# Storing the outputs of the last two quads plane by plane, from two DMA queues

## The chip, the cores and the metric

The kernel runs on one core of one Trainium2 chip. A core has five engines that run side by side, each with its own list of instructions in order: TensorE (PE in the profile, with PEld for its weight loads), VectorE (DVE), ScalarE (ACT), GpSimd (POOL) and SyncE (SP). Data goes between the chip's memory and the core through 16 DMA engines, which work off what SyncE's and ScalarE's queues hand them. The metric is the device time of one execution in microseconds, and lower is better.

## The reference

The input `x` is 128 samples of 64 channels by 1024 positions in float32; each sample has a style vector of 128. Four modulated convolutions of three taps are applied in turn (same length, upsampling by two with a blur, same length, blur and downsampling by two), and `x` is added to the result:

```python
def _layer(x, style, w, b, mw, mb, typ):
    s = style @ mw.T + mb
    weight = SCALE * w * s[:, None, :, None]
    demod = lax.rsqrt(jnp.sum(weight * weight, axis=(2, 3)) + EPS)
    weight = weight * demod[:, :, None, None]
    ...
out = x
for i, typ in enumerate(TYPES):        # same, upsample, same, downsample
    out = _layer(out, style, weights[i], biases[i], mod_w[i], mod_b[i], typ)
x = x + out
```

There is no nonlinearity between the layers, so away from the two ends of a sample all four are one convolution with its own weights for each sample.

## The kernel before

The kernel folds the four layers of a sample into one set of combined weights, built on TensorE from small products (`stage1`, `stage2`, `stage3`, lines 387 to 491), and then convolves each sample once. The three positions at either end of a sample are computed apart and leave by a store of their own (`Oe`, line 923).

Work is tiled by quads, four samples at a time, so there are 32 (`NQ`). Channels of two samples fill the 128 partitions, and two such pairs lie side by side. A sample's positions are split into three planes: plane `i` holds every third output, 340 of them. The convolution from three planes to three planes is done as five products instead of nine (`product`, line 579, and `conv0` to `conv4` that call it). They are accumulated in PSUM, in one pair of banks per quad (`psA`) and one that all quads share (`Y`), and VectorE puts them together (`sum1`, `sum2`, lines 627 to 641). Plane 1 is read from `y1w` in SBUF after `sum2`, plane 2 from `Y` after `conv4`, plane 0 from `psA` after `conv0`.

`output(q, i, s)` (line 651) scales plane `i` of pair `s`, adds the constant and writes it to the tile `o` of the quad in SBUF, on ScalarE (line 659) or VectorE (line 661). `store(q, s, planes, queue)` (line 663) is one DMA from `o` to the output, of as many planes as it is told; one plane of one pair is 170 KB, all three 510 KB. There are two `o` tiles, used in turn.

The order of work on each engine is the order in which the program is written: the schedule is a manual one, and the framework only adds the waits. The loop over quads begins at line 1101. An ordinary quad is convolved while the next quads' weights and inputs are prepared, and its two stores of 510 KB are issued by SyncE at the end of its turn (line 1224). The last two quads have branches of their own. Quad 30 is in the branch `n == NQ - 1` (line 1128): there planes 1, 2 and 0 of quad 30 are put out while `conv3`, `conv1` and `conv2` of quad 31 run in between. Quad 31 is in the branch `n == NQ` (line 1107), in which nothing is left to prepare; two of its outputs are given to VectorE to go beside ScalarE's.

Of the kernel before, what the change touches and what calls it, by code (L numbers as in the profile page):

```python
# [55 lines left out]
K = 3  # L56
# [7 lines left out]
def kernel(  # L64
# [9 lines left out]
    nc = tc.nc  # L74
# [8 lines left out]
    nc_v, nc_a, nc_g = nc.vector, nc.scalar, nc.gpsimd  # L83
# [344 lines left out]
    def stage2(q, pool=None, engs=(nc_a, nc_a), between=None):  # L428
        st = chain[q]
        ps = unit(pool or ps_w, f"psR{q}")  # L430
        for n, e in enumerate((-2, -1, 0, 1, 2, 3, 4, 5, 6)):
            if e % 2 == 0:
                a, lo, m = slice(1, 4), e // 2 + 1, 3
            else:
                a, lo, m = slice(4, 6), (e + 3) // 2, 2
            for r, rows in enumerate(HALF):
                for c, cols in enumerate(HALF):
                    src = st[c if r == 0 else 1 - c]
                    nc.tensor.matmul(  # L439
                        ps[r][cols, lo * C : (lo + m) * C],  # L440
                        E[rows, e + 2, :],
                        src[rows, a, :],
                        start=(n == 0),
                        stop=(n == 8),
                        skip_group_check=True,
                    )
        if between:
            between()
        rt = []
        for r in range(2):  # L450
            t = r_pool.tile([P, 7, C], F32, tag="R", name=f"R{q}_{r}")
            scaled_copy(
                engs[r], t.rearrange("c t o -> c (t o)"), ps[r][:, : 7 * C], tC[:, q, r : r + 1]
            )
            rt.append(t)
        chain[q] = rt
        return ps
# [79 lines left out]
    def t_tile(q, tag):  # L537
        if (q, tag) not in Ts:
            Ts[q, tag] = tpool.tile([P, 2, 1 + (tag != "T3"), PL], F32, tag=tag, name=f"{tag}_{q}")
        return Ts[q, tag]  # L540
# [31 lines left out]
    def in04(q, c):  # L572
        if q < NQ:
            t, g = t_tile(q, "T04"), Gs[q]
            a, b = g[:, c, :NJ], g[:, c, 2 * PL : 2 * PL + NJ]
            both = lambda v, step: bass.AP(v.tensor, v.offset, [list(v.ap[0]), [step, 2], [1, NJ]])
            nc_v.tensor_sub(t[:, c, :, :NJ], both(a, PL), both(b, 1))  # L577

    def product(q, m, ps, groups=range(K)):

        W, H_ = Wq[q]
        tag, i = SLOT[m]
        for g in groups:
            for s, rows in enumerate(HALF):
                for c, cols in enumerate(HALF):
                    if m in (0, 4):
                        w = W[rows, c, m // 2, g, :]
                    else:
                        w = H_[rows, m - 1, c, g, :]
                    nc.tensor.matmul(  # L590
                        ps[s][cols, :NB],
                        w,
                        Ts[q, tag][rows, c, i, g : g + NB],
                        start=(g == 0 and m == 3),
                        stop=(g == K - 1),
                        skip_group_check=True,
                    )
# [12 lines left out]
    def banks(q):  # L610
        return A[q] if isinstance(A[q], list) else [A[q][:, s] for s in range(2)]
# [31 lines left out]
    def conv4(q, *groups):  # L643
        product(q, 4, Y_banks, groups or range(K))

    def conv0(q, *groups):
        product(q, 0, banks(q), groups)
# [3 lines left out]
    def output(q, i, s, eng=nc_a):  # L651

        if q not in os:
            os[q] = opool.tile([P, 2, K, NB], F32, tag="o", name=f"o{q}")
        d3, add = td[:, q, s : s + 1], tb[:, q, s : s + 1]
        src = (banks(q)[s][:, :NB], y1w[q][:, s], Y[:, s, :NB])[i]
        dst = os[q][:, s, i]
        if eng is nc_a:
            nc_a.activation(dst, src, AF.Identity, bias=add, scale=d3)  # L659
        else:  # L660
            eng.tensor_scalar(dst, src, d3, add, op0=ALU.mult, op1=ALU.add)

    def store(q, s, planes=slice(0, K), queue=nc.sync):
        queue.dma_start(
            out[q, :, s, planes.start * NB : planes.stop * NB],
            os[q][:, s, planes].rearrange("c i j -> c (i j)"),
        )
# [108 lines left out]
    def zeros():  # L776
        for t in Ye:
            nc_g.memset(t[:, :, 0:1], 0.0)
            nc_g.memset(t[:, :, 7:8], 0.0)
        for t in Ue:  # L780
            nc_g.memset(t[:, :, 0:1], 0.0)
            nc_g.memset(t[:, :, 10:11], 0.0)
        for t in Ve:
            nc_g.memset(t[:, :, 0:2], 0.0)
            nc_g.memset(t[:, :, 10:12], 0.0)
        nc_g.memset(g1, 0.0)
# [314 lines left out]
    for q in range(NQ):  # L1101
        n, c, s = q + 1, q + 2, q + 3
        if q == 1:
            nc.sync.dma_start(Xe, x_ends)
        if q == 5:
            zeros()
        if n == NQ:
            conv4(q)
            for i in range(2):
                output(q, 2, i)  # L1110
            for i in range(2):
                output(q, 1, i, nc_v)
            for i in range(2):
                store(q, i, slice(1, 3))
            conv0(q, *range(K))
            for i, (eng, queue) in enumerate(zip(BOTH, (nc_a, nc.sync))):
                output(q, 0, i, eng)
                store(q, i, slice(0, 1), queue)
            break
        if c < NQ:  # L1120
            stage2(c)
        if n < NQ - 1:
            sum2(q)
        if n < NQ - 1:
            combine_a(n)
            combine_b(n)

        if n == NQ - 1:

            conv3(n, ps_w)  # L1130
            copy_m3(n)
            conv4(q, 0, 1)
            for i in range(2):
                output(q, 1, i)
            conv1(n)
            sum1(n)
            conv4(q, 2)
            for i in range(2):
                output(q, 2, i)
            in04(n, 0)  # L1140
            in04(n, 1)
            conv0(q, 0)
            conv2(n)
            conv0(q, 1, 2)
            sum2(n)
            for i in range(2):
                output(q, 0, i)
                store(q, i)
            continue

        conv4(q)
        if q == 0:
            var_matmul(PART[1], var_of(PART[1]), start=False)
            var_root(PART[1], var_of(PART[1]))
            var_inverse(PART[1])
            var_newton(PART[1])
            table_A(PART[1], dm[:, 2, PART[1]])
            for of in (table_C, vector_c0, table_3, vector_Da):
                of(PART[1])
        for i in range(2):  # L1160
            output(q, 2, i)
        if c < NQ:
            stage3(c, 0)
        conv3(n)
        copy_m3(n)
        in04(n, 0)
        in04(n, 1)
        if q:
            in3(c)
            in_g01(c, 0)  # L1170
            in_g01(c, 1)
        if c < NQ:
            stage3(c, 1)
        conv0(q, 0)
        conv1(n, 0)
        if q in SLOTS:
            slot(*SLOTS[q])
        elif s < NQ:
            stage1_a(s)
        conv1(n, 1, 2)  # L1180
        for i in range(2):
            output(q, 1, i)
        if q:
            in_g2(c)
            load(c + NX)
        if q and c < NQ - 1:
            in1(c, nc_g)
            in2(c, nc_g)
        if n == NQ - 2:
            combine_a(n + 1, lambda: sum1(n))  # L1190
            combine_b(n + 1)
        else:
            sum1(n)
        if q == 0:
            in_g01(c, 0)
            in_g01(c, 1)
        conv0(q, 1)
        if q in SLOTS:
            stage1_a(s)
        elif s < NQ:  # L1200
            stage1_b(s)
        conv0(q, 2)
        for i in range(2):
            output(q, 0, i)
        conv2(n, 0)
        if q in SLOTS:
            stage1_b(s, nc_v)
        extra(q, 0)
        extra(q, 1)
        if s + 1 < NQ:  # L1210
            scale3(s + 1)
        conv2(n, 1, 2)
        if n == NQ - 2:
            sum2(n)
            in1(n + 1, nc_v)
            in2(n + 1, nc_v)
        if q == 0:
            in_g2(c)
            in3(c)
            load(c + NX)  # L1220
            in1(c, nc_g)
            in2(c, nc_g)
        for i in range(2):
            store(q, i)
# [74 lines left out]
```

## Time and profile before

| | us |
|---|---|
| runs: median of 3 (lowest, highest) | 495.83 (495.58, 497.23) |
| the profiled execution | 496.51 |
| its span, first to last instruction | 494.7 |
| TensorE matmul busy | 481.8 |
| VectorE busy | 398.7 |
| ScalarE busy | 290.5 |
| GpSimd busy | 137.0 |

The profile is of one execution. Times inside it are microseconds from the start of its span; the execution's own time is 1.8 us longer than the span. Groups of instructions are named by the line of the kernel, the engine, the operation and what it writes and reads (`out<-o` is a store from the tile `o`). `SPq` and `ACTq` are the queues of SyncE and ScalarE: a DMA's row gives the time that its issue took there, and apart from it the time from issue to landing, when the last of the 16 DMA engines has reported its part. The DMA share is the mean busy share of the 16 engines. q1 carries what SyncE issues and q10 what ScalarE issues; the queues marked "instruction" carry program code to the engines.

### The profile page before, as it was taken

Reading aid. Unit: us, or ns where it says so; the run is one execution under the profiler, and the core shown is the slowest. Engines: PE = TensorE matmul, PEld = TensorE weight load, DVE = VectorE, ACT = ScalarE, POOL = GpSimd, SP = SyncE. Lnnn points to the kernel's source line nnn. Section 1 sums busy time; section 2 is a strip of 40 time slices with the busy share of each in tenths; the row PEclk is TensorE's granted clock in tenths of the full one; section 3 lists DMA queues with packets and bytes.
Section 4 is the critical chain, followed back from the end, with each engine's and each line's share of the span. In section 5 each row is a group of like instructions: output and inputs, shape, how many; then the busy total and the mean of one; then the engine's idle time right before and its main releaser. Section 6 shows DMA issues by size and latency. Waiting matters only on the chain.

```text
span 494.7 us, 22227 instructions
## 1 busy us (share of the span) xinstructions
PE 481.8 (97%) x10056; PEld 355.1 (72%) x10056; DVE 398.7 (81%) x704; ACT 290.5 (59%) x579; POOL 137.0 (28%) x164
## 2 busy tenths in 40 slices
PE   8999999999999999999999999999999999999994
PEld 6877687767777766767777777766766777777752
DVE  4986888798898869997768897759998768878783
ACT  5456646556565656556566556656555657566552
POOL 3544412344213223121223112223123323211200
PEclk9999999999999999999999999999999999999998
DMA  7220744443334442344443334442344442434224
GB/s 248 94 90 4 237 155 168 173 167 113 109 133 173 174 171 93 102 158 170 173 154 108 114 145 173 174 164 75 115 166 173 173 173 89 160 128 161 89 86 170
DMA packets 19727, 70.42 MB, mean 142 GB/s; under 512 B 2224, under 2 KB 2992, under 8 KB 19632
## 3 DMA queue, kind: packets, MB, share of 16 engines
q1 hardware_dynamic: 19408, 68.70, 39.0%
q8 instruction: 79, 1.29, 1.0%
q10 hardware_dynamic: 224, 0.29, 0.2%
q14 instruction: 16, 0.13, 0.1%
HBM read 35.36 MB, written 33.62 MB: 139 GB/s over the span
## 4 chain that ended last, share of the span: by engine, by line
PE 82%; DVE 11%; POOL 4%; issue 2%; ACT 1%; POOLq 0%; DVEq 0%
PE psA L590 37%; PE psR L439 14%; PE psW L480 13%; PE Y L590 9%; PE psS L369 5%; DVE G L501 3%; PE psE L820 2%; DVE H L501 2%; POOL T L565 1%; DVE T L577 1%; POOL T L570 1%; PE Y L169 1%; DVE Y L501 1%; DVE y L641 1%; DVE Wf L498 1%
## 5 line engine op out<-in xcount | busy, mean ns | idle before, releaser
L590 PE MATMUL psA<-T,H 64*64 64x340 f32 x2304 | 192.2, 446 | 0.7 <-DVE y L501 0.7
L565 POOL TENSOR_TENSOR T<-G 128x684 f32<-128x684 f32 x30 | 50.1, 1669 | 306.7 <-DVE G L501 266.6
L590 PEld LDWEIGHTS psA<-T,H 64*64 64x64 f32 x2304 | 92.8, 133 | 53.0 <-issue 6.7
L439 PE MATMUL psR<-S,E 64*64 64x192 f32 (+1 forms) x2304 | 88.0, 301 | 3.6 <-POOL S L425 2.3
L439 PEld LDWEIGHTS psR<-S,E 64*64 64x64 f32 x2304 | 77.3, 133 | 18.0 <-POOL S L425 7.6
L340 ACT ACTIVATE R<-psR,tC 128x448 f32<-128x448 f32 x63 | 36.6, 631 | 75.7 <-PE psR L439 73.9
L501 DVE SCALAR_TENSOR_TENSOR G<-X 128x688 f32<-128x688 f32 (+1 forms) x96 | 78.1, 866 | 0.0
L590 PE MATMUL psA<-T,Wf 64*64 64x340 f32 x768 | 74.0, 447 | 0.0
L501 DVE SCALAR_TENSOR_TENSOR y<-psA,m 128x680 f32<-128x680 f32 (+1 forms) x33 | 27.8, 845 | 46.8 <-PE psA L590 46.6
L340 ACT ACTIVATE Wf<-psW,t 128x384 f32<-128x384 f32 (+1 forms) x126 | 56.4, 498 | 11.5 <-PE psW L480 11.5
L480 PE MATMUL psW<-R,w0s 64*64 64x128 f32 (+1 forms) x1536 | 62.1, 287 | 0.4 <-ACT Wf L340 0.3
L590 PE MATMUL Y<-T,Wf 64*64 64x340 f32 x768 | 61.6, 446 | 0.4 <-DVE Y L501 0.3
L480 PEld LDWEIGHTS psW<-R,w0s 64*64 64x64 f32 x1536 | 51.1, 133 | 8.2 <-ACT Wf L340 1.2
L577 DVE TENSOR_TENSOR T<-G 128x684 f32<-128x684 f32 x64 | 52.7, 865 | 0.0
L659 ACT ACTIVATE o<-Y,tb,td 128x340 f32<-128x340 f32 x64 | 37.2, 631 | 23.4 <-ACT R L340 16.8
L570 POOL TENSOR_TENSOR T<-G 128x684 f32<-128x684 f32 x30 | 50.0, 1666 | 0.0
L369 PEld LDWEIGHTS psS<-wd,w2n 64*64 64x64 f32 x1160 | 38.5, 133 | 11.1
L659 ACT ACTIVATE o<-psA,tb,td 128x340 f32<-128x340 f32 x63 | 36.7, 634 | 14.9 <-PE psA L590 14.9
L590 PEld LDWEIGHTS Y<-T,Wf 64*64 64x64 f32 x768 | 31.8, 133 | 17.0 <-DVE Y L501 1.0
L340 ACT ACTIVATE S<-psS,tBn 128x256 f32<-128x256 f32 x58 | 24.4, 471 | 25.4 <-PE psS L369 25.3
L622 ACT COPY m<-psA 128x680 f32<-128x680 f32 (+1 forms) x33 | 23.3, 710 | 25.4 <-PE psA L590 25.4
L659 ACT ACTIVATE o<-y,tb,td 128x340 f32<-128x340 f32 x62 | 38.1, 668 | 0.0
(148 smaller groups left out, 529.2 us busy)
## 6 DMA issues: line engine op xcount, KB each, us to landing
X<-in_x SPq DMA_DIRECT2D x64, 516.0 KB, 4.5
out<-o SPq DMA_DIRECT2D x62, 510.0 KB, 4.4
out<-o SPq DMA_DIRECT2D x2, 340.0 KB, 4.4
Xe<-in_x_ends SPq DMA_DIRECT2D x1, 512.0 KB, 7.4
par<-in_params SPq DMA_DIRECT2D x2, 192.0 KB, 3.5
par_s<-in_params_s SPq DMA_DIRECT2D x1, 196.0 KB, 2.8
par<-in_params SPq DMA_DIRECT2D x2, 96.0 KB, 2.9
out<-Oe SPq DMA_DIRECT2D x1, 192.0 KB, 1.9
```

The source lines that it names most:

```text
L340: nc_a.activation(dst, src, AF.Copy, scale=f)
L369: nc.tensor.matmul(ps[r][cols, at * C : (at + n) * C], weight[rows], wd[c if r == 0 else 1 - c][rows, taps], start=first, stop=last, skip_ ...
L439: nc.tensor.matmul(ps[r][cols, lo * C : (lo + m) * C], E[rows, e + 2, :], src[rows, a, :], start=(n == 0), stop=(n == 8), skip_group_check ...
L480: nc.tensor.matmul(ps[r][cols, at : at + m * C], w0s[kind][rows, k, :], rt[c][rows, first : first + K * (m - 1) + 1 : K, :], start=(n == 1 ...
L501: nc_v.scalar_tensor_tensor(out, x, f, y, op0=ALU.mult, op1=op)
L565: eng.tensor_add(t[:, :, 0, :NJ], plane(g, 2), plane(g, 1))
L570: eng.tensor_sub(t[:, :, 1, :NJ], plane(g, 2), plane(g, 1))
L577: nc_v.tensor_sub(t[:, c, :, :NJ], both(a, PL), both(b, 1))
L590: nc.tensor.matmul(ps[s][cols, :NB], w, Ts[q, tag][rows, c, i, g : g + NB], start=(g == 0 and m == 3), stop=(g == K - 1), skip_group_check ...
L622: nc_a.copy(m3c[q][:, s], a)
L659: nc_a.activation(dst, src, AF.Identity, bias=add, scale=d3)
L820: nc.tensor.matmul(ps[r][cols, : HB * n].rearrange("c (b j) -> c b j", j=n), weight(i, r, c)[rows], moving(i, r, c)[rows], start=(i == 0), ...
```

## The change

In the branch of quad 30, planes 1 and 2 are stored as soon as both are written, and plane 0 alone at the end. In the branch of quad 31, plane 1 is put out and stored first in the program's order, one pair from SyncE's queue and one from ScalarE's; plane 2 is stored alone when it is written. Plane 0 of quad 31 goes as before. Before, quad 30 left in two stores of three planes, and quad 31 in two stores of two planes and two of one; now there are two stores of two planes and eight of one. No arithmetic is added or removed. TensorE, VectorE, GpSimd and ScalarE keep their instructions in the same order, except for one DMA issue that ScalarE gains ahead of its plane-2 outputs of quad 31.

```diff
         if n == NQ:
+            for i, queue in enumerate((nc.sync, nc_a)):
+                output(q, 1, i, nc_v)
+                store(q, i, slice(1, 2), queue)
             conv4(q)
             for i in range(2):
                 output(q, 2, i)
-            for i in range(2):
-                output(q, 1, i, nc_v)
-            for i in range(2):
-                store(q, i, slice(1, 3))
+                store(q, i, slice(2, K))
             conv0(q, *range(K))
             for i, (eng, queue) in enumerate(zip(BOTH, (nc_a, nc.sync))):
                 output(q, 0, i, eng)
@@
             conv4(q, 2)
             for i in range(2):
                 output(q, 2, i)
+                store(q, i, slice(1, K))
             in04(n, 0)
             in04(n, 1)
             conv0(q, 0)
@@
             sum2(n)
             for i in range(2):
                 output(q, 0, i)
-                store(q, i)
+                store(q, i, slice(0, 1))
             continue
```

## The prediction

> **What bounds the kernel now.** I read the page's head and its chain first, to see which engine carries the span. The last line is from the chain of waits in order of time, over the last 30 us.
>
> ```profile
> span 494.7 us, 22227 instructions
> PE 481.8 (97%) x10056; PEld 355.1 (72%) x10056; DVE 398.7 (81%) x704; ACT 290.5 (59%) x579; POOL 137.0 (28%) x164
> PE 82%; DVE 11%; POOL 4%; issue 2%; ACT 1%; POOLq 0%; DVEq 0%
> ...
> 488.30 0.63 DVE o L661
> ```
>
> TensorE is the bound for all but the end. The chain's last piece of arithmetic ends at 488.30 + 0.63 = 488.93, while the span is 494.7: 5.8 us pass in which nothing is computed. The edit touches nothing before 481 us, so this tail is the stage to price. Next I read the end of the waits of SyncE's queue, then the instructions of the kernel's closing line.
>
> ```profile
> SPq L1290 <- DMA out<-o: 4.3, 1, 4.3
> ...
> L1290 SPq EVENT_SEMAPHORE  x7: 17/28/4322, 489.3 to 494.7; - x7
> ```
>
> SyncE waits 4.32 us, from 489.34 to about 493.65, for the last store to land; the remaining 494.7 - 493.65 = 1.05 us is the closing handshake, which the edit leaves alone. So the span moves one for one with that landing. The stores' own rows (windows on the last two stores, on the two before them, on the pair of quad 30, and the lone side store) say why it takes so long:
>
> ```profile
> L664 ACTq DMA_DIRECT2D out<-o x1: 378/378/378, 488.9 to 488.9; - x1
> L664 SPq DMA_DIRECT2D out<-o x1: 332/332/332, 489.0 to 489.0; - x1
> DMA to landing us min/median/max: 4.5/4.6/4.7
> ...
> L664 SPq DMA_DIRECT2D out<-o x2: 401/588/776, 487.3 to 488.1; - x2
> ...
> L664 SPq DMA_DIRECT2D out<-o x2: 332/332/332, 485.2 to 485.7; - x2
> ...
> out<-Oe SPq DMA_DIRECT2D x1, 192.0 KB, 1.9
> ```
>
> A last store of 170 KB takes 4.5 to 4.7 us, though the side results' store of 192 KB, alone on the DMA engines, landed after 1.9. The difference is a queue: six stores (2 x 510, 2 x 340, 2 x 170 = 2040 KB of 1024 bytes) are issued within 3.8 us. The table of stretches shows the DMA engines (columns: stretch, length, busy time of PE, PEld, DVE, ACT, POOL, clock, DMA share, GB/s):
>
> ```profile
> 480.00:485.20 5.20, 5.13 (x75) 3.42 (x70) 4.31 (x9) 1.82 (x4) 0.00 (x0) 1.00 0.00 0
> 485.20:485.75 0.55, 0.55 (x13) 0.34 (x9) 0.55 (x3) 0.50 (x1) 0.00 (x0) 1.00 0.00 0
> ...
> 486.00:491.00 5.00, 2.22 (x32) 1.09 (x24) 0.63 (x1) 1.80 (x3) 0.00 (x0) 1.00 0.99 381
> 490.50:491.50 1.00, 0.00 (x0) 0.00 (x0) 0.00 (x0) 0.00 (x0) 0.00 (x0) 0.96 0.95 343
> 491.89:492.87 0.98, 0.00 (x0) 0.00 (x0) 0.00 (x0) 0.00 (x0) 0.00 (x0) 0.50 0.07 22
> 492.90:493.60 0.70, 0.00 (x0) 0.00 (x0) 0.00 (x0) 0.00 (x0) 0.00 (x0) 0.50 0.00 0
> ```
>
> From 480.0 to 485.75 they move next to nothing; from 486.0 to 491.0 they are full at 381 GB/s. Then from 491.89 to 492.87 their share is 0.07, about one engine of sixteen, carrying 22 GB/s x 0.98 us = 21.6 kB, a sixteenth of the last two stores: one engine runs over a microsecond behind the others. What made it late stands in the rows of the DMA queues, over 485.70 to 485.80 and over the span:
>
> ```profile
> q8 instruction: 1, 0.02, 90.9%
> ...
> q8 instruction: 79, 1.29, 1.0%
> q14 instruction: 16, 0.13, 0.1%
> ```
>
> One packet of program code starts in that 0.1 us; 90.9% of 16 engines x 0.1 us is 1.45 us on one engine. Its start is in the 23rd of 40 slices, 485.76, so this engine is free at 487.21 and has its share, 2040 KB/16 = 130.6 kB, done at 492.87: 5.66 us, 23 GB/s. The landing follows 0.78 us behind its last packet. That is the whole tail: a backlog, worked off last by the engine that fetched code.
>
> **The change, part by part.** The rows of ScalarE and VectorE that make the planes ready, in order of time:
>
> ```profile
> 480.97 1.16 ACT L659 ACTIVATE o<-Y,tb,td 128x340 f32<-128x340 f32 x2 [1.51 <-PE Y L590]
> 484.54 1.16 ACT L659 ACTIVATE o<-psA,tb,td 128x340 f32<-128x340 f32 x2 [2.41 <-PE psA L590]
> 485.16 0.82 DVE L661 TENSOR_SCALAR o<-y,td,tb 128x340 f32<-128x340 f32 x2
> 486.61 1.16 ACT L659 ACTIVATE o<-Y,tb,td 128x340 f32<-128x340 f32 x2 [0.91 <-ACT o L659]
> 488.24 0.63 ACT L659 ACTIVATE o<-psA,tb,td 128x340 f32<-128x340 f32 x1 [0.47 <-PE psA L590]
> ```
>
> 1. Quad 30, planes 1 and 2 (2 x 340 KB): plane 2 is ready at 480.97 + 1.16 = 482.13, and plane 1 was before it. The stores now issue at about 481.6 and 482.2 instead of with plane 0 at 485.20 and 485.73. The 0.8 us from issue to first packet is the time from 485.20 to 486.0; 696 kB at 381 GB/s take 1.83, so they run from 482.4 to 484.3 in the stretch that showed no traffic. SyncE was waiting there anyway. Matmuls, weight loads and outputs go on as before; their cover is that the matmuls already ran beside full DMA engines from 486.0 on.
>
> 2. Quad 30, plane 0 (2 x 170 KB): the issues stay at 485.20 and 485.73, with a third of the bytes.
>
> 3. Quad 31, plane 1 (2 x 170 KB): ready at 485.16 + 0.82 = 485.98, instead of waiting for plane 2 at 487.2 and 487.8. SyncE issues one behind its two others, 0.53 after 485.73, at 486.26; ScalarE issues the other at 486.0. Its issue is the one instruction added to a compute engine. Priced by the issues that ScalarE and SyncE show, it takes 0.38; the longest of all output issues took 1.08 (row below). Behind it stand ScalarE's plane-2 outputs, which began at 486.61, and then the last one, at 488.24 after 0.47 of idle time. An issue of 0.38 ends at 486.38 and costs nothing; one of 1.08 ends at 487.06, puts the outputs 0.45 back and eats the 0.47 to the last hundredths. I take zero, bound 0.05. Without that cover all of it would be on the end.
>
> ```profile
> L664 SPq DMA_DIRECT2D out<-o x65: 332/344/1080, 50.1 to 489.0; - x65
> ```
>
> 4. Quad 31, plane 2 (2 x 170 KB): issued at 487.27 and about 487.8 as it is ready. Plane 0: ScalarE at 488.91, SyncE at 488.96, as now. SyncE's two extra waits in front of it end at 488.2 at the latest.
>
> The bytes left behind the code packet are then 8 x 170 KB = 1360 KB, on the late engine 87.0 kB. Rows of one plane go slower than whole ones: 343 GB/s at share 0.95 is 22.6 GB/s for each engine, so 3.85 us, and from 487.21 the last packet ends at 491.06. Nothing holds it up on the way: the last stores' packets are there from 488.96 + 0.8 = 489.8, when this engine still has two stores' worth before it. Landing 0.78 later: 491.84, against 493.65. **The sum is -1.8 us.**
>
> Bounds. If that engine is not late at all, the last pair itself sets the end: the lone side store took 1.9 us, of which 196.6 kB / 385 GB/s = 0.5 were transfer, so 1.35 are fixed; 488.96 + 1.35 + 348 kB / 361 GB/s (0.96) = 491.3, a gain of 2.4. The mean code packet of that queue is 1.0% x 16 x 494.7 / 79 = 1.0 us, shorter than 1.45, so the gain is pulled towards this end rather than away. The other way: a second code packet (the smaller kind, 0.1% x 16 x 494.7 / 16 = 0.5 us) on the same engine leaves 1.3. I take 1.8, from the engine as it stood here. A fixed cost per store would come on top; the six stores here already fit their bytes (23 GB/s on the late engine, 22.6 with one-plane rows alone), so I take none.
>
> The profiled execution took 496.51 us, 1.8 around its span, so it would take 494.7. It stands 0.7 above the median of the runs, 495.83; the same sum on the median gives **494.0 us** (-0.36%).
>
> On this cost the Trainium skill speaks against the change. "DMA: Bandwidth & Descriptors", section "Bandwidth", says to batch transfers to a megabyte or more, and measures 0.95 us for 64 KB and 6.15 for 1 MB (loads issued from GpSimd); between them that is an estimated 0.6 us per transfer beside its bytes. The sum by it would be two more stores behind the code packet, 1.2 us, and a gain of 0.6. The trace here does not agree: with 0.6 each, the last two one-plane stores would have held the late engine for 1.2 us beside their bytes, and it took 0.98 with them. It is the third rival's rule, in a milder form.
>
> **The rivals.**
>
> *A part of the gain is lost, or it drowns.* An engine is late again at another moment, by 0.3 us or more beyond the 1.45, and 0.3 to 1.8 of the gain is gone: 494.3 to 495.8, by its middle 495.2. For it: code packets fall where they fall, and runs of one kernel already lie 495.58 to 497.23 apart, as wide as the gain. Against it: TensorE's code is untouched, and with it the place of this packet.
>
> *The change does not do what it says.* A store lands about 4.5 us after its issue whatever is queued; the last issues stay, and so does the time: 495.8. For it: the median of all the output stores is 4.4. Against it: those travel in pairs of 510 KB, mostly beside loads, and the lone store landed in 1.9.
>
> *A fixed cost per store: slower.* Place: the late engine's queue, between 487.21 and the end. Each of the eight stores costs c more than its bytes at the rates above, so the end moves by 8c against a gain of 1.8; at c = 0.23 the gain is gone, above it the kernel is slower, at 0.41 by 0.3%. The upper price is the 1.35 us of the lone store, if it could not overlap with the next one: 8 x 1.35 - 1.8 = 9 us, 504.8. Against it: the last two one-plane stores, one from each queue, passed the late engine in 0.98 us together, all included, and 0.96 is what I give a pair. At the smallest price that counts, c = 0.41, it would be 497.3.
>
> **How the numbers follow.** About 0.3% (1.5 us) is what a measurement here can tell from no change. The forecast (gain 1.5 to 2.4): 0.66; part of the gain lost: 0.24; no effect: 0.06; fixed cost: 0.04. The forecast's own range is 493.4 to 494.4. For 8 in 10 I go from 493.0 (gain 2.4 and 0.4 for the spread of runs) to 495.5, which takes in most of the lost gain. Faster by over 0.3%: 0.66; within: 0.30; slower: 0.04.
>
> **What would show it.** Right: traffic between 482.4 and 484.3; ScalarE's added issue done before 486.6 and its last output at 488.24 as before; issues of the last two stores at 488.9; from issue to landing 2.9 instead of 4.7; SyncE's last wait 2.5 instead of 4.32. Wrong: a later last output (the added issue held ScalarE), a landing still 4 us after issue with the queue empty (it was no backlog), or a new stretch with one busy engine long after the others (code fetched later).

## The result: faster by a fifth of a percent, half of what was forecast

| | before | after |
|---|---|---|
| median of 22 runs (lowest, highest), us | 496.40 (495.18, 497.79) | 495.17 (494.53, 496.47) |
| ratio after to before, 95% interval | | 0.9981 (0.9974 to 0.9989) |
| profiled execution, us | 496.51 | 494.94 |
| its span, us | 494.7 | 493.1 |

The ratio on record is a gain of 0.94 us on 496.4 (0.55 to 1.29); the two medians lie 1.23 apart, a quotient of 0.9975. The forecast was 1.8, with 1.5 to 2.4 as its own range. The gain is clear of zero, but it lies under the forecast's range and under the 0.3% that the prediction took as the least that can be told from no change. That 495.17 lies inside the wide range of absolute times, 493.0 to 495.5, says little.

The head of the profile after shows that nothing but the end has moved: all five engines do the same work, within 0.7 us. The arithmetic ends at the same moment too, by the last line of its chain of waits, in the second fence: 488.28 + 0.63 = 488.91, before 488.93.

```profile
span 493.1 us, 22234 instructions
PE 481.8 (98%) x10056; PEld 354.4 (72%) x10056; DVE 398.4 (81%) x704; ACT 290.6 (59%) x579; POOL 136.6 (28%) x164
```

```profile
488.28 0.63 DVE o L661
```

The rows of the last two stores of the profile after, and those of the other late stores between 485.1 and 488.5:

```profile
L664 ACTq DMA_DIRECT2D out<-o x1: 360/360/360, 488.9 to 488.9; - x1
L664 SPq DMA_DIRECT2D out<-o x1: 332/332/332, 488.9 to 488.9; - x1
DMA to landing us min/median/max: 3.0/3.1/3.2
...
L664 SPq DMA_DIRECT2D out<-o x5: 332/406/1152, 485.2 to 487.9; - x5
L664 ACTq DMA_DIRECT2D out<-o x1: 354/354/354, 486.0 to 486.0; - x1
```

The last store lands 3.2 us after its issue instead of 4.7. One number stands out: an issue on SyncE that took 1.152 us, against 0.33 for most (the longest of the late ones before took 0.776). It is the plane-1 store that stands right behind ScalarE's added one. The stretches of the profile after (columns as in the prediction):

```profile
482.40:484.30 1.90, 1.90 (x30) 1.30 (x22) 1.44 (x4) 0.00 (x0) 0.00 (x0) 1.00 0.95 367
486.00:487.00 1.00, 1.00 (x20) 0.69 (x16) 0.00 (x0) 0.41 (x1) 0.00 (x0) 1.00 0.88 310
487.00:487.50 0.50, 0.50 (x16) 0.29 (x11) 0.00 (x0) 0.50 (x2) 0.00 (x0) 1.00 1.02 348
487.50:488.00 0.50, 0.50 (x12) 0.10 (x4) 0.00 (x0) 0.25 (x1) 0.00 (x0) 1.00 0.51 174
488.00:489.00 1.00, 0.19 (x4) 0.00 (x0) 0.63 (x1) 0.63 (x1) 0.00 (x0) 1.00 0.98 343
489.00:490.00 1.00, 0.00 (x0) 0.00 (x0) 0.00 (x0) 0.00 (x0) 0.00 (x0) 1.00 0.59 203
490.00:491.00 1.00, 0.00 (x0) 0.00 (x0) 0.00 (x0) 0.00 (x0) 0.00 (x0) 0.76 0.75 263
491.00:491.65 0.65, 0.00 (x0) 0.00 (x0) 0.00 (x0) 0.00 (x0) 0.00 (x0) 0.50 0.06 21
```

Quad 30's early planes do travel from 482.4 to 484.3. But from 486 on the DMA engines are no longer full: 0.51 for half a microsecond at 487.5 and 0.59 in all of 489 to 490, where before the share was 0.99 throughout. The second gap is only a wait for the last pair: its issues are at 488.9, and first packets come 0.8 us behind an issue. And one engine is still last: from 491.0 to 491.65 the share is 0.06, about one engine of sixteen.

### The profile page after: what moved, and what is told of

Same layout as the page of the kernel before. It is cut to its first block, busy times and chain, and to the rows that moved or that the text cites. A ratio compares the mean times of both kernels' runs of the same rounds, so it can differ in the third digit from the quotient of the medians.

```text
span 493.1 us, 22234 instructions
## 1 busy us (share of the span) xinstructions
PE 481.8 (98%) x10056; PEld 354.4 (72%) x10056; DVE 398.4 (81%) x704; ACT 290.6 (59%) x579; POOL 136.6 (28%) x164
## 3 DMA queue, kind: packets, MB, share of 16 engines
q8 instruction: 79, 1.29, 1.1%
## 4 chain that ended last, share of the span: by engine, by line
PE 82%; DVE 11%; POOL 4%; issue 2%; ACT 1%; POOLq 0%; DVEq 0%
PE psA L590 37%; PE psR L439 14%; PE psW L480 13%; PE Y L590 9%; PE psS L369 5%; DVE G L501 3%; PE psE L820 2%; DVE H L501 2%; POOL T L565 1%; DVE T L577 1%; POOL T L570 1%; PE Y L169 1%; DVE Y L501 1%; DVE y L641 1%; DVE Wf L498 1%
```

## The experiments

Two theories stood against each other. *Backlog*, the prediction's: the end moves with the bytes that are queued behind the code packet. *Feeding*: many small stores reach the DMA engines more slowly than their bytes, because issues are held or two queues disturb each other.

The arithmetic itself ends anywhere from 488.3 to 490.6 us in the profiles of these kernels, though none of the edits but the last product's order and the start's warm-up touches it. That scatter is as large as the effect, so beside the timed ratio I read each trace's *tail*: from the end of the last output to the last landing. It is the end of the last output in the chain of waits, the issue right behind it, and the "DMA to landing" of that issue. Each ratio compares runs on one chip; the tails are single profiles, and the three groups of experiments below ran on three chips.

### Each half alone, one queue, and the change again

The half in quad 30 alone is the change with quad 31's branch left as it was:

```diff
         if n == NQ:
-            for i, queue in enumerate((nc.sync, nc_a)):
-                output(q, 1, i, nc_v)
-                store(q, i, slice(1, 2), queue)
             conv4(q)
             for i in range(2):
                 output(q, 2, i)
-                store(q, i, slice(2, K))
+            for i in range(2):
+                output(q, 1, i, nc_v)
+            for i in range(2):
+                store(q, i, slice(1, 3))
```

> Only the half of the change in quad 30: planes 1 and 2 leave early, plane 0 at the end; quad 31 is stored as before the change (two stores of two planes, two of one, six in all behind 485 us instead of eight). Backlog theory (the end moves with the bytes queued behind the code packet, 1360 KB as in the full change): the same time as the full change, the last landing near 491.8 to 492.2, about 1.5 us less than before in the profile. Feeding theory (eight small stores reach the DMA engines more slowly than their bytes, and two issuing queues get in each other's way): faster than the full change by 0.3 us or more, and the DMA share stays at 0.95 or above between 487 and 490.

The half in quad 31 alone is the kernel before with the opposite edit:

```diff
         if n == NQ:
+            for i, queue in enumerate((nc.sync, nc_a)):
+                output(q, 1, i, nc_v)
+                store(q, i, slice(1, 2), queue)
             conv4(q)
             for i in range(2):
                 output(q, 2, i)
-            for i in range(2):
-                output(q, 1, i, nc_v)
-            for i in range(2):
-                store(q, i, slice(1, 3))
+                store(q, i, slice(2, K))
```

> Only the half of the change in quad 31: plane 1 early, one pair from SyncE and one from ScalarE, plane 2 alone; quad 30 leaves whole at the end as before. Backlog theory: 2040 KB behind the code packet as before, so no difference from before (within 0.3 us). Feeding theory: the small stores cost time and buy nothing, 0.3 to 0.8 us slower than before.

One queue for both plane-1 stores:

```diff
-            for i, queue in enumerate((nc.sync, nc_a)):
+            for i, queue in enumerate((nc.sync, nc.sync)):
```

> The full change with both plane-1 stores of quad 31 issued by SyncE; ScalarE issues only its last store. Backlog theory: the same as the full change within 0.2 us. Feeding theory with the two queues in each other's way: the long issue on SyncE (1.15 us in the full change) is gone, issues follow at 0.53 us, and the end comes 0.3 to 0.6 us earlier than in the full change. If the small rows alone are the limit, the same as the full change.

> The full change once more, on the chip of the three halves: 0.9 to 1.3 us less than before. In its trace the theory of backlog expects the same places of the waits as in the first profile; if the long SyncE issue beside ScalarE's and the gaps of the DMA share at 487.5 and 489.5 are chance, they are gone or elsewhere.

| | ratio to before (95%) | tail, us |
|---|---|---|
| half in quad 30 | 0.9964 (0.9951 to 0.9977) | 3.22 |
| half in quad 31 | 1.0003 (0.9991 to 1.0016) | 4.97 |
| full change, one queue | 0.9984 (0.9971 to 0.9997) | 3.52 |
| full change again | 0.9980 (0.9969 to 0.9992) | 3.70 |

The half in quad 31 wins nothing, as the backlog theory expected (2040 KB stay behind the code packet); the 0.3 to 0.8 us of loss that the feeding theory expected is neither shown nor excluded by its time, whose interval goes up to 0.8, and its tail is 0.27 longer than the longest of before. The half in quad 30 carries the gain. Its 1.8 us are more than the full change's 0.94, as the feeding theory expected, but see its repetition below. No issue is held in it (0.33 us each). The theory's other sign, a DMA share of 0.95 or more between 487 and 490, did not come: it was 0.31 from 487 to 488, where the half's stores of two planes had only just been issued. The second queue is not what disturbs: with SyncE alone the time is the same, and a long issue is there too (1.13 us, on the fourth store in a row).

In the repetition of the full change the held issue is longer. Its rows of the late stores, and its stretches around the hold:

```profile
L664 SPq DMA_DIRECT2D out<-o x5: 332/384/1516, 485.5 to 488.6; - x5
L664 ACTq DMA_DIRECT2D out<-o x1: 354/354/354, 486.3 to 486.3; - x1
```

```profile
487.00:488.00 1.00, 1.00 (x20) 0.65 (x16) 0.00 (x0) 1.00 (x2) 0.00 (x0) 1.00 0.89 310
488.00:488.50 0.50, 0.50 (x8) 0.00 (x0) 0.00 (x0) 0.11 (x1) 0.00 (x0) 1.00 0.07 19
488.50:489.00 0.50, 0.06 (x4) 0.00 (x0) 0.35 (x1) 0.41 (x1) 0.00 (x0) 1.00 0.94 318
```

From 488.0 to 488.5 the share is 0.07, one engine of sixteen: fifteen have run dry and one works. So the gap behind a held issue is no chance. What was still open was whether the number of small stores holds the issue, or the one late engine.

### The floor, the number of stores, and the order of the last product

```diff
         if n == NQ:
-            for i, queue in enumerate((nc.sync, nc_a)):
+            for i in range(2):
                 output(q, 1, i, nc_v)
-                store(q, i, slice(1, 2), queue)
...
                 output(q, 2, i)
-                store(q, i, slice(2, K))
...
             for i in range(2):
                 output(q, 0, i)
-                store(q, i, slice(0, 1))
             continue
```

> Leaves work out: plane 0 of quad 30 and planes 1 and 2 of quad 31 are computed but never stored, so only the last pair of stores stands behind 485 us. It measures the end without any backlog. By the bounds of the prediction the last landing comes 2.3 us after SyncE's last issue and the time is 2.4 us under before. If the two last stores are worked off one behind the other, as the half in quad 30 showed (landings 0.55 us apart, the second 3.19 after its issue), 2.8 to 3.2 after the issue and 1.6 to 2.0 under before, the same as that half.

Split, from the half in quad 30:

```diff
             for i in range(2):
-                store(q, i, slice(1, 3))
+                store(q, i, slice(1, 2))
+                store(q, i, slice(2, 3))
```

> The half in quad 30 alone, but each of quad 31's two stores of two planes is split into two stores of one plane, issued one behind the other at the place of the whole one: same bytes, eight stores behind 485 us instead of six, rows of 1360 bytes instead of 2720, and nothing leaves earlier. Backlog theory: as the half in quad 30 alone (about 1.8 us under before). Feeding theory: issues held for 0.4 us or more, gaps in the DMA share, and 0.4 to 0.9 us slower than that half, about where the full change is.

By side, from the half in quad 30; `product` gets an argument that sorts its order of groups and pairs by pair:

```diff
-            conv0(q, *range(K))
-            for i, (eng, queue) in enumerate(zip(BOTH, (nc_a, nc.sync))):
+            product(q, 0, banks(q), range(K), True)
+            for i, (eng, queue) in enumerate(((nc_v, nc.sync), (nc_a, nc_a))):
```

> The half in quad 30 alone, with the last product of quad 31 ordered pair by pair instead of group by group: the first pair's plane 0 is finished about 0.9 us earlier, put out on VectorE and stored by SyncE, so that the last store goes alone, from ScalarE. If the last two stores being worked off one behind the other sets the end, 0.5 to 0.9 us faster than the half in quad 30 alone. If the landing behind the last issue is what it is whatever goes before, no difference.

> The half in quad 30 alone once more, beside the three above: 1.3 to 2.2 us under before. Where its code packet comes late or long in the trace, the backlog theory expects one engine behind the others at the end again; the feeding theory expects no held issue of SyncE in either case.

| | ratio to before (95%) | tail, us |
|---|---|---|
| floor: last pair alone | 0.9974 (0.9960 to 0.9987) | 3.09 |
| quad 30's half, quad 31 split | 0.9985 (0.9970 to 0.9999) | 3.64 |
| quad 30's half, last product by side | 0.9976 (0.9963 to 0.9989) | 2.89 |
| quad 30's half again | 0.9982 (0.9967 to 0.9997) | 3.19 |

The floor kernel leaves out the other six late stores. It is the surprise. The end of its chain, and then the rows of its last pair:

```profile
488.48 0.63 DVE o L661
```

```profile
L664 ACTq DMA_DIRECT2D out<-o x1: 379/379/379, 489.1 to 489.1; - x1
L664 SPq DMA_DIRECT2D out<-o x1: 332/332/332, 489.1 to 489.1; - x1
DMA to landing us min/median/max: 3.0/3.0/3.1
```

With nothing at all in front of them the last two stores still need 3.0 and 3.1 us to land. The prediction had 2.3 for this; of the two outcomes expected before this run, the second came. So no store moved out of the way can win more than about 4.7 - 3.1 = 1.6 us here, and quad 30's half, with tails of 3.22 and 3.19, is already there. The Trainium skill, "DMA: Bandwidth & Descriptors", section "Anatomy of one DMA", gives 2.0 us plus the bytes at 436 GB/s (measured on another issuing path); for the pair's 348 kB, taken as one transfer, that is an estimated 2.8, nearer to the 3.1 measured here than the prediction's bound.

The split was meant to have the same bytes at the same times as quad 30's half, but it has not. Plane 1 is written before plane 2, so the first of the split stores no longer waits for plane 2. SyncE issues it at 487.7, half a microsecond before ScalarE begins plane 2, where the half's store of two planes comes 1.5 us behind the store before it. That issue is held for 1.34 us:

```profile
L664 SPq DMA_DIRECT2D out<-o x2: 332/837/1342, 487.3 to 487.7; - x2
488.16 1.16 ACT L659 ACTIVATE o<-Y,tb,td 128x340 f32<-128x340 f32 x2 [0.91 <-ACT o L659]
```

So the tail, 0.42 to 0.45 longer than the half's, is no price for the number of stores alone. By side, the last store goes alone, and the tail is 0.30 shorter than quad 30's half, less than the 0.5 expected.

The timed ratios do not resolve all this. Quad 30's half came out at 0.9964 and then at 0.9982, in intervals that overlap, so that it is faster than the full change is not shown by its times; its tails (3.22 and 3.19 against 3.25 and 3.70) only suggest it. By side and quad 30's half both beat the kernel before; neither is told from the full change by its time.

### The kernel before again, and the code packet moved away

> The kernel before once more, for a second sample of its end: from the end of the last output to the last landing 4.70 us in its first profile. Backlog theory with the code packet: 4.4 to 4.9 again, one engine last by about 1.1 us at the landing, since the packet's place in TensorE's code does not change. If the first profile was an unlucky one, 3.7 to 4.2, which would by itself explain most of what the timed gain lacks.

> The kernel before a third time, for the spread of its tail: 4.4 to 4.9 by the backlog theory with the code packet; anywhere from 3.6 to 4.9 if the packet's length (0.9 to 1.9 us in the profiles so far) sets it, in step with that length.

For the two kernels with a shifted start, one edit in the warm-up at the start, made in the kernel before and in the full change:

```diff
-    zeros_to_y(2, 256)
-    zeros_to_y(2, 384)
+    zeros_to_y(20, 32)
```

> The kernel before, with the warm-up products at the start cut into more and narrower ones (20 sets of 32 columns instead of 4 of 256 and 384): 128 more instructions in TensorE's code, so its code packets fall about 4.5 us earlier against the work, and none falls between 485 and the end. Backlog theory with the code packet: the 15 punctual engines set the end, tail from the last output to the landing 3.6 us instead of 4.7. If the packet has nothing to do with the late engine, 4.7 again.

> The full change with the same narrower warm-up products. Without a late engine SyncE's issues should not be held (0.33 to 0.45 us instead of 1.15 and 1.52), and the tail should be at its floor, 3.0 to 3.2 us. Against the kernel before with the same start that is only 0.4 to 0.6 us, so most of what the change wins would be the late engine's backlog. If held issues come from the number of small stores and not from the late engine, they are held here too, and the tail stays 3.3 to 3.7.

The second profile of the kernel before: the end of its chain, SyncE's last store with the landings of the last pair, and the code packet, in the rows of the DMA queues over the 0.1 us from 487.05:

```profile
489.86 0.63 DVE o L661
```

```profile
L664 SPq DMA_DIRECT2D out<-o x1: 335/335/335, 490.5 to 490.5; - x1
DMA to landing us min/median/max: 3.8/4.0/4.2
```

```profile
q8 instruction: 1, 0.02, 73.6%
```

And the same of its third profile (the packet over the 0.1 us from 487.80):

```profile
489.99 0.63 DVE o L661
```

```profile
L664 SPq DMA_DIRECT2D out<-o x1: 332/332/332, 490.6 to 490.6; - x1
DMA to landing us min/median/max: 4.3/4.4/4.5
```

```profile
q8 instruction: 1, 0.02, 54.8%
```

Tails of 4.24 and 4.49: the 4.70 of the first profile is the longest of three, and their mean is 4.48. The 4.24 lies between the two ranges that were expected of it. The tail does not follow the packet's length alone, which was 1.45, 1.18 and 0.88 us in that order (a share of 16 engines over 0.1 us, as in the prediction): the shortest packet has the middle tail. The full times of these two executions were 497.69 and 497.97.

What the landing does follow is the end of the packet. By their slices the packets start at 485.76, 487.09 and 487.86, so they end at 487.21, 488.27 and 488.73 (rounded). The last store lands 6.42, 6.46 and 6.38 us after that. The prediction's sum for the kernel before, 5.66 us of work and 0.78 to the landing, makes 6.44. A tail is long where the packet ends late against the last output.

With the start shifted, the packet is out of the way. In the kernel before with that start, it stands in the 0.1 us from 480.85, and none between 485 and 494:

```profile
q8 instruction: 1, 0.02, 57.2%
```

Its stretches, the end of its chain, and its last stores:

```profile
486.50:491.50 5.00, 2.21 (x32) 1.09 (x24) 0.63 (x1) 1.80 (x3) 0.00 (x0) 1.00 1.01 388
491.50:492.25 0.75, 0.00 (x0) 0.00 (x0) 0.00 (x0) 0.00 (x0) 0.00 (x0) 1.00 0.56 200
492.25:493.00 0.75, 0.00 (x0) 0.00 (x0) 0.00 (x0) 0.00 (x0) 0.00 (x0) 0.50 0.00 0
```

```profile
488.79 0.63 DVE o L661
```

```profile
L664 SPq DMA_DIRECT2D out<-o x1: 332/332/332, 489.5 to 489.5; - x1
DMA to landing us min/median/max: 3.4/3.5/3.6
```

The engines are full until 491.5 and all done by 492.25; no engine is left behind, and the tail is 3.62, as expected (3.6). The full change with that start, its late stores and its last pair:

```profile
L664 SPq DMA_DIRECT2D out<-o x5: 332/332/410, 486.8 to 489.4; - x5
...
L664 SPq DMA_DIRECT2D out<-o x1: 332/332/332, 490.5 to 490.5; - x1
DMA to landing us min/median/max: 2.9/3.0/3.1
```

And its stretches:

```profile
488.00:489.00 1.00, 1.00 (x21) 0.58 (x16) 0.00 (x0) 0.83 (x2) 0.00 (x0) 1.00 0.96 331
489.00:490.00 1.00, 0.77 (x12) 0.18 (x4) 0.14 (x1) 0.53 (x2) 0.00 (x0) 1.00 1.00 329
```

The same ten stores, and no issue is held: 0.41 us at most, where it was 1.15 and 1.52. The DMA share has no gap in these two microseconds (it dips at 491, before the packets of the last pair), and the tail is 3.11, the floor. These four profiles, the kernel before twice and the two with the shifted start, are from one chip. So it is the packet, with the engine that it makes late, that holds the issues, and not the number of small stores.

The traces say when. Five profiles have an issue of SyncE longer than 1.1 us: the change, its repetition, one queue, the split, and the second profile of the kernel before, with six stores:

```profile
L664 SPq DMA_DIRECT2D out<-o x1: 1354/1354/1354, 487.3 to 487.3; - x1
```

Each began 0.2 to 0.4 us after the start of the packet, and ended about 0.4 us after the packet's end. In the two profiles of quad 30's half, in by side and in the third of the kernel before, no issue of SyncE began within the packet and none was held. The small stores of the change put an issue there. ScalarE's issue, which also fell there, was not held (0.354 us).

The ratios to the kernel before are 0.9980 (0.9964 to 0.9996) for the shifted start alone and 0.9977 (0.9958 to 0.9995) with the full change: with the code packet out of the end, the kernel before is faster by about as much as by the whole change (by 0.86 us in its tail), and with that done the change takes off another 0.5 us of tail that the times cannot show. The edit changes the warm-up as well, so for the packet's part the tails are the evidence, one profile each.

## Why the prediction was right and where it failed

1. *The tail is a backlog, worked off last by the engine that fetched code.* Right, and now shown: without the packet the kernel before loses 0.6 to 1.1 us of tail and no engine is late; with the packet, it lands 6.4 us after the packet's end in three profiles, as the sum had it; with fewer bytes behind the packet the tail shrinks.

2. *Quad 30's planes 1 and 2 travel unseen from 482.4 to 484.3.* Right, to the tenth, and this half is the gain: 3.2 us of tail against 4.48.

3. *ScalarE's added issue costs nothing.* Right: 0.354 us at 485.98, with the last outputs where they were.

4. *"Nothing holds it up on the way."* This is the step that failed. The sum let the late engine work through the 1360 KB without a break, so that the last store would land 3.85 + 0.78 = 4.63 us after the end of the code packet. The packet of the change, in the 0.1 us from 485.65, and of its repetition, in those from 486.00:

```profile
q8 instruction: 1, 0.02, 74.6%
```

```profile
q8 instruction: 1, 0.02, 96.4%
```

They start at 485.70 and 486.06 and end at 486.89 and 487.60; the landings are at 492.16 and 492.97, 5.27 and 5.37 us later. So counted from the packet's end the change is worth 1.1 us (6.4 to 5.3) and not 1.8. On the way the fourth store in a row was held on SyncE for 1.15 us (1.52 in the repetition) and the other fifteen engines ran dry. But whether the hold is what took the 0.7 us is not shown. In the change the stores behind it were issued by 487.9, where 487.8 was forecast, and the last two on time (in the repetition the former came 0.4 us behind the forecast and the latter on time, counted from the last output). The one engine at work was slow itself, too: it moved 19 GB/s from 488.0 to 488.5 in the repetition, where the sum had 22.6. The prediction's cover was also thinner than it says: by its own rate, at 489.8 the engine had 0.3 us of work in front of the last pair, not two stores' worth.

5. *The bound of 2.3 us for the last pair, taken from the lone side store.* Mis-sized: 3.0 to 3.1 in the floor. The sum did not use this bound, but its own end, 2.9 us after the last issue, lies under the floor; a gain of 1.8 on a tail of 4.7 was not to be had with the two last stores as they are. The side store is no measure for a store of a plane.

6. *The tail of before, 4.70.* One profile's value, 0.22 above the mean of three, since its packet ended latest against the last output. The prediction noted that its execution was 0.7 slower than the median, but carried over its tail whole.

7. *The closing handshake stays.* Off by 0.2 in the change's favour: from the landing to the end of the span it took 1.08 us before and 0.90 after. SyncE's waits for the last stores ended in four steps, the longest 1.9 us, where before one of 4.3 stood first and the others followed it.

```profile
SPq L1291 <- DMA out<-o: 2.8, 4, 1.9
```

Put together: the mean tail goes from 4.48 to 3.48 (of 3.25 and 3.70), 1.0 us, and the handshake gives 0.18: 1.2, which is what the medians show (1.23) and within the interval of the ratio (0.55 to 1.29). Of the 0.8 that the tail falls short of the forecast, 0.2 is the long tail that was taken for before, and 0.6 is the end after, which came later than the sum had it; the floor alone makes 0.2 of that. With three and two profiles that scatter by 0.45, these parts are rough.

Of the rivals, the first gave the number that came (495.2), but by luck: its reason, an engine late at another moment, is not the one found. The second, 4.5 us to the landing whatever is queued, is refuted by the floor's 3.1; that something stays whatever is queued was right. The third, a fixed cost for each store, is refuted by the shifted start, where the same ten stores, eight of them of one plane, end at the floor. The Trainium skill's rule on batching ("DMA: Bandwidth & Descriptors", section "Bandwidth"), which the prediction weighed against the change, gave an estimated gain of 0.6, nearer to the measured 0.94 than the forecast's 1.8; but the shifted start shows no cost that every transfer carries.

Open: what the held issue costs at the end, and what slowed the late engine. Shorter holds also come outside the packet: in the kernel before, SyncE's third store was held for 0.78 us right behind it, with two of 510 KB in front, and in the half in quad 31 issues took 0.72 to 1.07. Neither bytes nor stores alone give one limit. Why a plane's store needs a microsecond more to land than the side store wasn't tried either.

## What to carry to other kernels

Before moving stores forward at the end of a kernel, measure the floor: the time from the last issue to its landing with nothing in front. Here it was two thirds of the tail. Take out of the last microseconds what can be moved whole, as quad 30's planes were; cutting quad 31's stores smaller won nothing. And look at what else uses the DMA engines just then, since one packet of code cost about as much as all the stores that the change moved. Where the effect is a microsecond and the runs scatter by three, compare the stretch itself in several traces.

## What the runs showed of the hardware that was not expected

One DMA engine that is late can hold up the issue of a store that is spread over all sixteen: an issue of 0.33 us took up to 1.52 when it began while that engine was reading a code packet, and for half a microsecond fifteen engines stood idle with a finished plane waiting (share 0.07). The landing of the last store then kept a fixed distance from the packet's end, 6.4 us in three profiles of the kernel before and 5.3 in two of the change. Two stores of 170 KB, alone, need 3.0 and 3.1 us to land, while a store of 192 KB from another tile landed in 1.9. And a code packet's place can be shifted by cheap instructions hundreds of microseconds earlier: 128 more at the start moved its start from about 3 us before the end of the last output (2.8 to 3.4) to 8.5 before it, and the tail from 4.48 to 3.62.
